# Edge-product tiles reordered by two engines in turn, and another pace for the edge scores in a four-layer graph network

## The chip, the cores and the metric

The kernel runs on one core of a Trainium2 chip. Its time is the device time in microseconds of one execution, here the median of three runs. The core has a matrix engine (TensorE, "PE" in the profile; its weight loads are "PEld"), a vector engine (VectorE, "DVE"), a scalar engine (ScalarE, "ACT"), a general engine (GpSimd, "POOL"), which here issues gathers and scatters as indirect DMAs, and SyncE ("SP"), which issues plain DMAs. Each engine works through its own queue in order. Tensors are laid over 128 partitions.

## The reference

Sixteen batches of 1024 nodes with 256 features pass through four layers over one adjacency matrix with few entries (about 17 a row). Everything is float32.

```python
# layer 0: a score for each edge, then sums over the edges
pre_u = einsum('bud,dk->buk', h, W1[:d]); pre_v = einsum('bvd,dk->bvk', h, W1[d:])
hidden = relu(pre_u[:, :, None, :] + pre_v[:, None, :, :] + b1)
S = sigmoid(einsum('buvk,ko->buvo', hidden, W2)[..., 0] + b2[0])
a = einsum('buv,bud->bvd', S * A, h)
m = einsum('uv,bud->bvd', A, h) * h
z = beta1*h + beta2*(a @ Wa + ba) + beta3*(m @ Wm + bm)
# layer 1
x = z + relu(einsum('ij,bjd->bid', A, z) @ W.T + b)
# layers 2 and 3 (attention, each with its own weights)
feats = x @ W1.T; f1 = feats @ W2 + b2
coefs = softmax(leaky_relu(f1[:, :, None] + f1[:, None, :]) + A, axis=-1)
x = coefs @ feats + bias2 + x
```

## The kernel before

The 16 batches are worked on in four groups of four (`GB = 4`). Node tiles have 128 rows (`NT = 8`).

**Edge scores.** Rather than score all 1024 × 1024 pairs, the kernel lists up to 32 neighbours of each node and scores those alone. `score_steps` (L717) is a generator with 608 steps after its first eight: a group has 8 node tiles × 16 slots and 6 extra tiles × 4 slots, so 152 steps. One step takes a tile of 128 × 1024 numbers (128 edges, four batches, 256 features each). GpSimd gathers it (L708, issued four steps ahead), VectorE adds the other side of the edge (L825) and applies relu and the weights (L827), and ScalarE sums each batch's 256 numbers (four operations, L831). After the last slot of a tile the sigmoid follows (L840 to L844), and its results wait in a list from which later steps scatter them, one or two a step (L713), into a dense array in DRAM, where the four batches of a pair of nodes lie side by side. L825 is `paced`: it waits until TensorE has done the product six before the place in the program where it stands.

**How the steps are dealt out.** `Side.along` (L888) runs a main generator, which yields nominal microseconds of TensorE work, and for each of them adds `PACE[stage]` to a debt. For each whole unit owed it issues one score step. The stages are `free` (work that needs no scores), `edges`, `one` (layer 1), `fronts` (projections of the attention layers) and `sums` (their weighted sums). Before a group's edge stage the program issues whatever steps are missing until that group is `finished`.

**The edge stage** (`with_edges`, L1120) multiplies the dense scores by each batch's transformed nodes (`hw`). It runs four column blocks `v` of 256 target nodes, and in each eight source tiles `ut`. For one tile SyncE loads `gd`, 128 × 256 nodes × 4 batches (512 KB, `load_gd`, four buffers), in which the batch is the innermost index. ScalarE copies it to `gc` with the batch outermost (L1129, two buffers, a read that hops four numbers each time), and TensorE runs eight products, which the profile shows as 16 matmul records. The eight sums of a block fill all eight PSUM banks. At the end of the block VectorE adds them to `z` (L1152, eight operations of 128 × 256), which frees the banks for the next block. A tile yields 3.4 nominal us (1 in the first block of group 0). In group 0 this stage also loads and exponentiates the adjacency (L1118). The first tiles of a group's edge stage are loaded ahead by `soon` (L1396) in the last sums of the group before.

**The layers of a group** (`group_layers`, L1355): layer 1 for two pairs of batches, then for each batch and attention layer a front (L1004, eight yields of 0.86) and two halves of sums (L1085, each eight yields of 1.7 and one of 1.2). A sums tile needs a VectorE operation `m` (L1099). The end of a sums half in the last layer reads four banks through L1325, L1326 and L1328, and only then are these banks free. Group 3's layers run with no score steps left; two of its four batches use lists for part of layer 1 (L1207, L1242, L1244).

The instructions of each engine are put in order when the program is built, by a scheduler that orders what is ready in its own estimate of the times; so the order on an engine isn't the order of the text. In group 2 at 2064.1 us, for example, L825 of a step runs ahead of a `gc` copy (2066.4 us), while that step's L831 follows it (2068.4 us).

Of the kernel before, what the change touches and what calls it, by code (L numbers as in the profile page):

```python
# [14 lines left out]
AF = mybir.ActivationFunctionType  # L15
# [5 lines left out]
BUFS = 2  # L21


PACE = dict(free=0.26, edges=0.225, one=0.288, fronts=0.255, sums=0.255)
SLOTS = 32
FIRST = 16
EXTRA = SLOTS - FIRST
# [16 lines left out]
def after(tc, ins, others, kind, why):  # L44
    dep = mybir.DependencyInfo(kind, mybir.DependencyReason.DATA)
    for o in others:
        tc.add_manual_dep(ins.ins, o.ins.name, dep, reason=why)
# [23 lines left out]
def gnn_stack_kernel(  # L71
# [27 lines left out]
    nc = tc.nc  # L99
# [13 lines left out]
    def bank():  # L113
        return psum[-1].tile([P, HN], F32, tag="bank", name="bank")
# [8 lines left out]
    def paced(ins, back=6):  # L123


        if recent:
            after(tc, ins, [recent[max(0, len(recent) - back)]], mybir.DependencyClass.Sync, "keeps pace")
        return ins

    def product(*args, **kw):  # L130
        recent.append(nc.tensor.matmul(*args, **kw))  # L131
        del recent[:-BACK]
        return recent[-1]
# [554 lines left out]
    with tc.If(listed > 0) as arm:  # L688
        with ExitStack() as stack:
# [192 lines left out]
            class Side:  # L882
# [4 lines left out]

                def along(self, main, pace=PACE):  # L888
                    for us in main:
                        self.owed += us * pace[doing[0]]  # L890
                        while self.owed >= 1:
                            self.owed -= 1
                            next(self.steps, None)
# [10 lines left out]
            def load_gd(g, v, ut, **pace):  # L904
                view = dense[g % BUFS][:DUMP].rearrange("(t p v) b -> t p v b", p=P, v=N)
                gd = gd_pool.tile([P, QN, GB], F32, tag="gd", name="gd")
                ins = nc.sync.dma_start(gd, view[ut][:, v * QN : (v + 1) * QN, :])
                put[g].before(paced(ins, **pace))
                return gd
# [207 lines left out]
            def exponential(jt):  # L1117
                paced(nc.scalar.activation(ea[:, jt, :], ea[:, jt, :], AF.Exp), 16)  # L1118

            def with_edges(g, hw, z):  # L1120

                doing[0] = "edges"
                for v in range(N // QN):
                    cols = slice(v * QN, (v + 1) * QN)
                    acc = [[bank() for _ in range(DH)] for _ in range(GB)]
                    for ut in range(NT):
                        gd = first_gd.pop(0) if first_gd else load_gd(g, v, ut, back=BACK)
                        gc = gc_pool.tile([P, GB, QN], F32, tag="gc", name="gc")
                        paced(nc.scalar.activation(gc, gd.rearrange("p n i -> p i n"), AF.Copy), 16)  # L1129
                        for i in range(GB):  # L1130
                            for eh in range(DH):
                                product(
                                    acc[i][eh][:, :QN], hw[i][:, ut, eh * P : (eh + 1) * P], gc[:, i, :],
                                    start=ut == 0, stop=ut == NT - 1,
                                )
                        if z_loads and ut % 2 == 0:
                            load, i = z_loads.pop(0)
                            paced(load(i), 12)
                        if (to_load or to_exp) and ut % 2 and v:
                            if v > 1 and to_exp:  # L1140
                                exponential(to_exp.pop(0))
                            if to_load:
                                jt = to_load.pop(0)
                                paced(nc.sync.dma_start(ea[:, jt, :], adjT_d[jt]), 16)
                                to_exp.append(jt)
                        yield 3.4 if g or v else 1
                    if v == N // QN - 1:
                        while to_exp:
                            exponential(to_exp.pop(0))
                    for i in range(GB):  # L1150
                        for eh in range(DH):
                            nc.vector.scalar_tensor_tensor(  # L1152
                                z[i][:, eh, cols], acc[i][eh][:, :QN], zbias[:, eh : eh + 1], z[i][:, eh, cols],
                                ALU.add, ALU.add,
                            )
# [245 lines left out]
            def far_ahead(z, main):  # L1401
# [6 lines left out]
                def slots():  # L1408
                    nonlocal gone
                    for us in itertools.chain(rest, main):  # L1410
                        gone += us
                        yield us * (0.68 if gone < 82 else 0.61)

                far.along(slots(), dict.fromkeys(PACE, 1))
                for _ in far.steps:
# [4 lines left out]
            for g in range(NGR):  # L1420
                hw, z = loaded.pop(0)
                while g not in finished:
                    next(side.steps)
                side.along(with_edges(g, hw, z))
                if g < NGR - 1:
                    side.along(group_layers(g, z))
                else:
                    for _ in far_ahead(z[2:], pair_layers(g * GB, z[:2], layer_one(z[:2]))):
                        pass
                    for _ in pair_layers(g * GB + 2, z[2:], from_lists(z[2:], msg)):  # L1430
                        pass
# [131 lines left out]
```

## Time and profile before

| | us |
|---|---|
| median of three runs (3133.77 to 3150.67) | 3143.56 |
| the profiled execution | 3123.2 |
| its span, first to last instruction | 3121.5 |
| TensorE matmuls busy | 3074.8 |
| VectorE busy | 2352.6 |
| ScalarE busy | 1945.1 |
| GpSimd busy | 1878.9 |

The mean granted TensorE clock was 0.998. The stages follow one another: work without scores up to about 942 us, then for each group its edge stage and its layers; group 0's edges begin at 942.1, group 1's at 1495.5, group 2's at 2045.3, group 3's at 2598.0 us. The 608 score steps run from 143.5 to 2547.8 us (first and last start of L825).

A row of the group view names line, engine, operation, what is written and read, shape and count; behind the bar stand busy time and mean ns of one, and then the engine's idle time ahead of these operations with what ended it. In the view of one tile's instructions a row gives duration as least/median/greatest in ns, and the first and last start. A row of the waits gives who waited for whom, total us, how often, and the longest. In the timeline a row is start, us, engine, line; like instructions close together are merged.

### The profile page before, as it was taken

To read this page: it belongs to the slowest core of one execution; us is meant where nothing else is said; L and a number is where in the kernel's file an instruction comes from. 1 tells how busy PE (TensorE), PEld (TensorE's weight loads), DVE (VectorE), ACT (ScalarE), POOL (GpSimd) and SP (SyncE) were. 2 spreads that over 40 slices of the span, in tenths; PEclk is the share of its full clock that TensorE was granted. 3 is DMA by queue.
4 is the path that set the end of the run, shared out by engine and by line. 5 is a ranking of instruction groups with operands and counts; after the bars stand their busy time and mean duration, and the time that the engine had idled before them with its cause. 6 is when DMAs were issued, how large, how long until landed. Compare 5 with 4: busy or idle time off the path is not lost. (4 is left out here: it accounts for less than half of the span.)

```text
span 3121.5 us, 39024 instructions
## 1 busy us (share of the span) xinstructions
PE 3074.8 (99%) x11954; PEld 2179.2 (70%) x11954; DVE 2352.6 (75%) x3183; ACT 1945.1 (62%) x6520; POOL 1878.9 (60%) x1483
## 2 busy tenths in 40 slices
PE   9999999999999999999999999999999999999999
PEld 5544555545547756888875688888568888858888
DVE  7887777768774678999667899966789982157844
ACT  3345565656667876787887677788667764414242
POOL 1156787777664577777666776766777770076600
PEclk9999999999999999999999999999999999999999
DMA  9998898888889776568877665887765565485500
GB/s 321 331 331 310 270 313 260 273 242 253 254 290 331 229 214 202 156 185 285 285 233 207 209 165 171 266 284 232 219 206 164 159 207 166 132 262 156 164 2 28
DMA packets 288420, 699.96 MB, mean 224 GB/s; under 512 B 46141, under 2 KB 141178, under 8 KB 281034
## 3 DMA queue, kind: packets, MB, share of 16 engines
q0 software_dynamic: 128224, 387.80, 42.5%
q1 hardware_dynamic: 132538, 258.46, 23.7%
q10 hardware_dynamic: 27440, 51.13, 4.3%
q8 instruction: 96, 1.57, 0.2%
q14 instruction: 122, 1.00, 0.1%
HBM read 565.83 MB, written 131.41 MB: 223 GB/s over the span
## 5 line engine op out<-in xcount | busy, mean ns | idle before, releaser
L831 ACT ACTIVATE z<-z 128x256 f32<-128x256 f32 x2432 | 979.0, 406 | 574.1 <-DVE z L827 549.0
L825 DVE TENSOR_TENSOR z<-z,u 128x1024 f32<-128x1024 f32 x608 | 738.9, 1220 | 374.8 <-PE bank L131 262.4
L131 PE MATMUL bank<-feats,m 128*128 128x257 f32 x4096 | 909.0, 380 | 0.7 <-ACT st L1325 0.5
L708 POOL DMA_INDIRECT z<-v_d,slot_v x512 | 662.2, 1293 | 376.0 <-ACT z L831 208.1
L131 PEld LDWEIGHTS bank<-feats,m 128*128 128x128 f32 x4096 | 769.4, 190 | 111.2 <-ACT st L1325 1.3
L713 POOL DMA_INDIRECT dense_d<-gt,slot_at x512 | 674.5, 1317 | 184.4 <-issue 130.3
L827 DVE SCALAR_TENSOR_TENSOR z<-z,w2r 128x1024 f32<-128x1024 f32 x608 | 737.3, 1219 | 9.0
L131 PE MATMUL bank<-gc,hw 128*128 128x256 f32 x2048 | 451.8, 382 | 15.6 <-ACT gc L1129 10.5
L831 ACT ACTIVATION_READ_ACCUMULATOR z<-z 128x1 f32 x2432 | 461.6, 190 | 0.0
L131 PE MATMUL bank<-adj_sb,h 128*128 128x512 f32 x1024 | 442.3, 592 | 3.3 <-ACT st L333 2.0
L131 PEld LDWEIGHTS bank<-gc,hw 128*128 128x128 f32 x2048 | 386.6, 190 | 80.2 <-ACT gc L1129 20.7
L1099 DVE SCALAR_TENSOR_TENSOR m<-rho,tau,adj_sb 128x512 f32<-128x512 f32 x512 | 375.8, 742 | 65.6 <-PE bank L131 62.7
L131 PE MATMUL bank<-adjT_in,y 128*128 128x512 f32 (+1 forms) x960 | 403.4, 581 | 6.0 <-DMA adjT_in<-adjT_d 5.9
L131 PEld LDWEIGHTS bank<-adj_sb,h 128*128 128x128 f32 x1024 | 194.3, 190 | 242.7 <-issue 237.5
L131 PEld LDWEIGHTS bank<-adjT_in,y 128*128 128x128 f32 x960 | 182.0, 191 | 221.0 <-issue 203.8
L131 PE MATMUL bank<-w,hT 128*128 128x512 f32 (+1 forms) x1024 | 334.9, 487 | 0.0
L1129 ACT ACTIVATE gc<-gd 128x1024 f32<-128x1024 f32 x128 | 264.7, 2069 | 88.4 <-PE bank L131 74.9
L131 PEld LDWEIGHTS bank<-w,hT 128*128 128x128 f32 x1024 | 194.8, 191 | 141.5 <-issue 118.4
L131 PE MATMUL bank<-g_wT,z 128*128 128x257 f32 x1024 | 231.4, 380 | 1.6 <-ACT st L1325 1.1
L131 PEld LDWEIGHTS bank<-g_wT,z 128*128 128x128 f32 x1024 | 191.8, 190 | 33.2 <-issue 3.1
L708 POOL DMA_INDIRECT z<-v_d,x_node x96 | 124.2, 1294 | 128.6 <-ACT z L831 96.6
L1152 DVE SCALAR_TENSOR_TENSOR z<-bank,zbias,z 128x256 f32<-128x256 f32 x128 | 54.6, 480 | 111.7 <-PE bank L131 111.4
(168 smaller groups left out, 2379.4 us busy)
## 6 DMA issues: line engine op xcount, KB each, us to landing
gd<-dense_d SPq DMA_DIRECT2D x128, 512.0 KB
dense_d<-zero ACTq DMA_DIRECT2D x64, 512.0 KB
adjT_in<-adjT_d SPq DMA_DIRECT2D x112, 256.0 KB
h<-in_x_dram SPq DMA_DIRECT2D x19, 1024.0 KB
u_d<-st SPq DMA_DIRECT2D x64, 256.0 KB
v_d<-st SPq DMA_DIRECT2D x64, 256.0 KB
hw_d<-st SPq DMA_DIRECT2D x64, 256.0 KB
u<-u_d POOLq DMA_DIRECT2D x32, 512.0 KB
```

The source lines that it names most:

```text
L131: recent.append(nc.tensor.matmul(*args, **kw))
L708: return nc.gpsimd.indirect_dma_start(out=dst, out_offset=None, in_=src[:], in_offset=bass.IndirectOffsetOnAxis(ap=at, axis=0), **how,)
L713: return nc.gpsimd.indirect_dma_start(out=dst[:], out_offset=bass.IndirectOffsetOnAxis(ap=at, axis=0), in_=src, in_offset=None,)
L825: paced(nc.vector.tensor_tensor(z, z, u, ALU.add))
L827: nc.vector.scalar_tensor_tensor(zk, zk, 0.0, w2r[:, None, :].to_broadcast([P, GB, D]), ALU.max, ALU.mult)
L831: nc.scalar.activation(zk[:, c, :], zk[:, c, :], AF.Copy, accum_out=s[:, k, c : c + 1])
L1099: nc.vector.scalar_tensor_tensor(m, r[:, cols], ta[:, kt : kt + 1], ea[:, kt, cols], ALU.max, ALU.mult)
L1129: paced(nc.scalar.activation(gc, gd.rearrange("p n i -> p i n"), AF.Copy), 16)
L1152: nc.vector.scalar_tensor_tensor(z[i][:, eh, cols], acc[i][eh][:, :QN], zbias[:, eh : eh + 1], z[i][:, eh, cols], ALU.add, ALU.add,)
```

## The change

Three of the five paces change, and the copy from `gd` to `gc` is made by VectorE for odd source tiles and by ScalarE for even ones. The wait that the copy carries (`paced(..., 16)`) stays the same.

```diff
-PACE = dict(free=0.26, edges=0.225, one=0.288, fronts=0.255, sums=0.255)
+PACE = dict(free=0.26, edges=0.255, one=0.288, fronts=0.265, sums=0.235)
...
                         gd = first_gd.pop(0) if first_gd else load_gd(g, v, ut, back=BACK)
                         gc = gc_pool.tile([P, GB, QN], F32, tag="gc", name="gc")
-                        paced(nc.scalar.activation(gc, gd.rearrange("p n i -> p i n"), AF.Copy), 16)
+                        by_batch = gd.rearrange("p n i -> p i n")
+                        if ut % 2:
+                            paced(nc.vector.tensor_copy(gc, by_batch), 16)
+                        else:
+                            paced(nc.scalar.activation(gc, by_batch, AF.Copy), 16)
```

## The prediction

> **What bounds the kernel now.** I read the page first, then the four runs of the edge product ("gc" matmuls) by their first and last start, then busy time by stage, then who waits for gc, and last VectorE's timeline at one turn of the column loop.
>
> ```profile
> PE 3074.8 (99%) x11954; PEld 2179.2 (70%) x11954; DVE 2352.6 (75%) x3183; ACT 1945.1 (62%) x6520; POOL 1878.9 (60%) x1483
> ```
>
> TensorE is the bound, but matmuls overlap in this count, so stalls hide in the 99%. The edge stages show them: each has the same 512 matmul records.
>
> ```profile
> L131 PE MATMUL bank<-gc,hw x512: 379/379/483, 942.1 to 1062.5; 128*128 128x256 f32 x171
> L131 PE MATMUL bank<-gc,hw x512: 379/379/483, 1495.5 to 1611.2; 128*128 128x256 f32 x171
> L131 PE MATMUL bank<-gc,hw x512: 379/379/634, 2045.3 to 2164.7; 128*128 128x256 f32 x171
> L131 PE MATMUL bank<-gc,hw x512: 379/379/382, 2598.0 to 2708.3; 128*128 128x256 f32 x171
> ```
>
> Lengths are 120.4, 115.7, 119.4 and 110.3 us. Group 3, with no score steps left, runs unhindered: 110.3/32 = 3.45 us for each node tile. The others lose 10.1 + 5.4 + 9.1 = 24.6 us. That is nearly all that this change can win.
>
> ```profile
> core 0: us, PE busy (x) PEld busy (x) DVE busy (x) ACT busy (x) POOL busy (x), PEclk, DMA share, GB/s
> 1063.00:1495.00 432.00, 431.04 (x1806) 328.73 (x1805) 396.26 (x541) 315.60 (x1190) 322.76 (x236) 1.00 0.69 209
> 1524.00:1611.00 87.00, 86.93 (x399) 74.83 (x399) 59.60 (x74) 82.11 (x187) 47.78 (x41) 1.00 0.81 260
> 2075.00:2165.00 90.00, 88.89 (x409) 76.74 (x408) 60.53 (x73) 83.22 (x189) 51.04 (x42) 1.00 0.82 263
> ```
>
> In the attention layers (first line) VectorE is 92% busy, yet TensorE idles 1 us: nothing is to be won there. In the edge stages ScalarE is the full engine (94%), VectorE has 32% free.
>
> ```profile
> L1129 ACT ACTIVATE gc<-gd 128x1024 f32<-128x1024 f32 x128 | 264.7, 2069 | 88.4 <-PE bank L131 74.9 <-DMA gd<-dense_d 12.8 <-ACT gc L1129 0.5
> L831 ACT ACTIVATE z<-z 128x256 f32<-128x256 f32 x2432 | 979.0, 406 | 574.1 <-DVE z L827 549.0 <-DVE share L1272 10.2 <-DVE mT L353 10.1
> L825 DVE TENSOR_TENSOR z<-z,u 128x1024 f32<-128x1024 f32 x608 | 738.9, 1220 | 374.8 <-PE bank L131 262.4 <-DMA z<-v_d,slot_v 62.7 <-ACT z L831 14.7
> L827 DVE SCALAR_TENSOR_TENSOR z<-z,w2r 128x1024 f32<-128x1024 f32 x608 | 737.3, 1219 | 9.0
> L1152 DVE SCALAR_TENSOR_TENSOR z<-bank,zbias,z 128x256 f32<-128x256 f32 x128 | 54.6, 480 | 111.7 <-PE bank L131 111.4
> L1078 ACT ACTIVATE rho<-rho 128x1024 f32<-128x1024 f32 x32 | 33.4, 1044 | 0.0
> L1242 DVE TENSOR_SCALAR msg<-z,slot_a 128x512 f32<-128x512 f32 x6 | 2.9, 486 | 0.4 <-PE bank L131 0.3
> ```
>
> The gathering read costs ScalarE 2069 ns against 1044 ns for a plain tile of that size. A score step is 1.22 + 1.22 = 2.44 us of VectorE and about 1.7 us of ScalarE (four times 0.41 us, the accumulator reads mostly beside). Who waits for gc:
>
> ```profile
> PE bank L131 <- ACT gc L1129: 10.5, 12, 2.2
> PEld bank L131 <- ACT gc L1129: 20.7, 31, 2.6
> PE bank L131 <- DVE st L1328: 4.3, 2, 2.8
> ```
>
> **Where the 24.6 us lie.** 4.3 us wait for L1328 and 0.7 for L1325, the end of the sums before, which frees banks; the granted clock was 0.94 over 30 us of group 2 (1.8 us). Three gaps of 2.18, 1.44 and 0.94 us (at 958, 963 and 1520 us) have ScalarE idle ahead of the copy: gd had not landed, so 4.6 us are the DMA's. This leaves 13 us that a busy ScalarE can answer for; I count 11.
>
> [...] L1242 needs 486 ns for 512 elements[...]. [...] Here every read of gc hops 16 bytes; no such large VectorE read is in this trace, ScalarE's doubling is the nearest. [...] The L1242 rows beside running gathers keep their 486 ns[...].
>
> **The change, part by part.**
>
> *Pace.* A step is issued for each 1/pace of a stage's nominal us. Edges: 4 × 8 × 3.4 = 108.8 nominal us, so 24.5 steps become 27.7 (+3.3). Sums: 16 × 14.8 = 236.8, times −0.020 = −4.7. Fronts: 64 × 0.86 = 55, times 0.01 = +0.6. A group ends some 1 step behind, group 0 (only 89.6 nominal us of edges) 1.5. All 608 steps still end within group 2, and each group's scores are complete well before its tiles load (group 2's last scatter goes 8 steps ahead, it was 10). So no forced run of steps appears. Relief in the sums is worth nothing, as TensorE doesn't stall there.
>
> *ScalarE in the edges.* A pair of tiles takes 6.91 us. Before: 2 × 2.07 + 1.53 × 1.7 = 6.7 us (97%; measured 94%). After: 2.07 + 1.73 × 1.7 = 5.0 us (73%). Its lateness goes: −11 us.
>
> *VectorE in the edges.* Before: 1.53 × 2.44 + 0.96 (L1152: eight of 0.48 in each eight tiles) = 4.7 us a pair (68%, as measured). After: 1.73 × 2.44 + 0.96 + c = 5.2 + c, with c the new copy. [...] it is 1.2 us as L827, plus ScalarE's extra of about 1.0 us: 2.2 us, the upper bound. [...] 1.25 us, which I take. A pair is then 6.4 of 6.91 us: it fits, hardly. Behind the copy queue only score steps, themselves held to TensorE's place; mid-block it starts about 0.5 us into the tile before its use and has 1.7 us to spare.
>
> *Where it doesn't fit.* The first copy of a column block after the prefetched one (tile 9, 17, 25: all odd, all VectorE's) meets the eight L1152 that free the banks:
>
> ```profile
> 1524.46 0.91 DVE L1152 SCALAR_TENSOR_TENSOR z<-bank,zbias,z 128x256 f32<-128x256 f32 x2 [4.85 <-PE bank L131]
> 1525.32 1.23 DVE L825 TENSOR_TENSOR z<-z,u 128x1024 f32<-128x1024 f32 x1
> 1526.46 0.48 DVE L1152 SCALAR_TENSOR_TENSOR z<-bank,zbias,z 128x256 f32<-128x256 f32 x1
> 1526.86 1.22 DVE L827 SCALAR_TENSOR_TENSOR z<-z,w2r 128x1024 f32<-128x1024 f32 x1
> 1527.99 2.04 DVE L1152 SCALAR_TENSOR_TENSOR z<-bank,zbias,z 128x256 f32<-128x256 f32 x5
> ```
>
> Tile 8 began at 1527.3 (two tiles after the gap at 1520); the last of these ends at 1530.03, 2.7 us in. A copy behind them ends at 2.7 + 1.25 = 3.95 us, 0.5 us late for 3.45; a copy ahead of them delays the last bank (due 3.0 us in) to 3.95, 0.9 us late. Nine such turns: 4.5 to 8.5 us, I take 6. It could be nothing if copy and steps change places.
>
> *DMA.* Three more steps in an edge stage add three gathers of 512 KB to a stage at a share of 0.81 to 0.88; the waits for gd may grow by 0 to 3 us: +1.
>
> Sum: −11 + 6 + 1 = −4 us on the profiled run's own 3123.2 us (span 3121.5, 1.7 around it): 3119. The runs' median is 20.4 us above that profile; moved alike, it comes to 3143.6 − 4 = 3139.
>
> **The rivals.**
>
> *A, faster.* Turns cost nothing, the stalls at the ends of sums go too since fewer steps crowd VectorE there (5 us), and the 20 us by which usual runs exceed the profile are partly the same lateness. For it: ScalarE at 94%, the only engine TensorE waits for here. Against: 6.4 us of DMA and clock stay. −11 − 5 − 5 = −21: 3122.
>
> *B, slower.* The strided copy on VectorE is slow. Above c = 6.91 − 5.2 = 1.7 us VectorE becomes the edges' bound. At 2.2 us a pair overruns by 0.5 us, 48 pairs in three groups: 24 us; turns add 2.7 + 2.2 − 3.45 = 1.45 × 9 = 13 us; less the 11 won: +26, 3169. For it: ScalarE's doubling[...]. Against: L1242's rate.
>
> *C, the new pace misplaces steps* against ends of sums, ±5 us by chance; it lies in the likeliest case's own range, 3129 to 3150.
>
> **How the numbers follow.** No change that can be told (a measurement of this kernel tells about 0.5%, 16 us): 0.42. A: 0.28. B: 0.30. The range 3118 to 3167 reaches nearly to A's and B's ends and leaves out about 2 in 10.
>
> **What would show it.** Right: VectorE's gc near 1.25 us, edge stages of about 114, 115 and 117 us, waits for ScalarE's gc near nothing, waits for L1152 or VectorE's gc at tiles 8, 9, 16, 17, 24, 25. Wrong: c above 1.7 us, VectorE near 100% in the edges, stages longer than before (B); or stages of 111 to 113 us (A); or new idle time of TensorE in sums or ahead of an edge stage.

## The result, and the profile after

The changed kernel takes 3129.74 us (median of 22 runs, 3120.36 to 3140.83); the kernel before, measured beside it, 3140.8 us (22 runs). The ratio is 0.9966, 95% interval [0.9954, 0.9977]. Repeated twice beside the experiments, the same kernel gave 0.9995 [0.9984, 1.0007] and 0.9997 [0.9988, 1.0005]. So the gain is 0.3% in one comparison and none that can be told in two: no change beyond 0.5%, as forecast. The kernel before itself had medians of 3140.8, 3129.1, 3126.0 and 3126.0 us in the four comparisons of this study, so kernels are compared below only by their ratio to the kernel before in the same comparison.

The busy times of the changed kernel, from the page:

```profile
PE 3071.5 (98%) x11954; PEld 2181.0 (70%) x11954; DVE 2422.3 (78%) x3247; ACT 1821.7 (58%) x6456; POOL 1894.7 (61%) x1483
```

ScalarE lost 123 us of work, VectorE gained 70. The span is 3122.0 us against 3121.5: in these two profiled executions nothing was won as a whole. Yet the stages moved. Edge product, changed kernel: the four stages one after the other, then the two kinds of copy (ns least/median/greatest, first and last start):

```profile
L131 PE MATMUL bank<-gc,hw x512: 379/379/797, 942.4 to 1063.2; 128*128 128x256 f32 x171
L131 PE MATMUL bank<-gc,hw x512: 379/379/483, 1496.6 to 1611.1; 128*128 128x256 f32 x171
L131 PE MATMUL bank<-gc,hw x512: 379/379/483, 2042.9 to 2157.1; 128*128 128x256 f32 x171
L131 PE MATMUL bank<-gc,hw x512: 379/379/792, 2594.6 to 2706.4; 128*128 128x256 f32 x171
...
L1133 ACT ACTIVATE gc<-gd x64: 2015/2084/2128, 934.6 to 2696.5; 128x1024 f32<-128x1024 f32 x64
L1131 DVE COPY gc<-gd x64: 1070/1116/1221, 945.0 to 2699.9; 128x1024 f32<-128x1024 f32 x64
```

Lengths are 120.8, 114.5, 114.2 and 111.8 us. Against the unhindered 110.3 the first three lose 18.6 us (24.6 before). Group 3, which lost nothing before, now loses 1.5. The copy costs VectorE 1.12 us.

Group 3's 1.5 us are the granted clock. It stood at 0.50 for 3.4 us just as the stage began, and its products started 0.43 us apart instead of 0.215 (the columns are explained at the next view; PEclk is the third number from the end):

```profile
2594.10:2597.50 3.40, 2.94 (x7) 2.41 (x8) 2.96 (x7) 1.49 (x5) 0.00 (x0) 0.50 1.01 367
```

The clock's record has other stretches at 0.50, of 3.4 or 6.8 us; in the edges of all profiles here each begins within 2 us of a wait of TensorE of 1 us or more. The changed kernel has one from 959.1 us (tile 4 of group 0, beside a wait of 2.9 us), the kernel before one from 2055.9 us (beside a wait of 2.8 us). One of 3.4 us costs 1.5 to 1.7 us, and the losses given below contain them.

Busy time by stage, changed kernel, edges of groups 1 and 2:

```profile
core 0: us, PE busy (x) PEld busy (x) DVE busy (x) ACT busy (x) POOL busy (x), PEclk, DMA share, GB/s
1497.00:1612.00 115.00, 112.52 (x515) 96.93 (x515) 97.13 (x113) 80.44 (x243) 85.73 (x64) 1.00 0.86 279
2043.00:2158.00 115.00, 112.88 (x517) 97.01 (x516) 98.56 (x115) 81.15 (x250) 86.95 (x66) 1.00 0.90 293
```

ScalarE is down from 94% to 70%, VectorE up from 68% to 85%; the DMA share of group 2 has risen to 0.90. Who makes TensorE wait in the edge product, over the whole changed kernel:

```profile
PEld bank L131 <- ACT gc L1133: 13.5, 9, 3.4
PE bank L131 <- ACT gc L1133: 10.2, 8, 3.2
PEld bank L131 <- DVE gc L1131: 6.1, 7, 1.7
PE bank L131 <- DVE gc L1131: 3.2, 4, 1.3
PEld bank L131 <- DVE z L1156: 1.2, 3, 0.7
```

The 10.2 us look like the 10.5 of before, but they are others. In the timelines I sorted the tiles by how late their first product starts (over 0.215 us after the product before it) and by what the copying engine did since `gc` became free. Where it sat idle until `gd` had landed I count 7.0 us (3.0 of them at tile 4 of group 0; 0.8 at tile 30 of group 1, where `gd` is only the likeliest reading); one wait of 1.2 us has ScalarE busy; 3.2 us stand ahead of group 3, which had no wait before. Counted in the same way the kernel before had 5.9 us for `gd` and 6.9 for a busy ScalarE (9.7 and, now, 1.3 for ScalarE with the small delays of a tile's other products).

Three further places changed. In group 2 the wait for the end of the sums (L1328, now L1332) is 0.2 us instead of 4.3. At the turns of the column loop VectorE's copy is late. And group 3 begins late. First a turn, on VectorE's timeline of the changed kernel, group 0, tile 17:

```profile
1000.74 0.92 DVE L1156 SCALAR_TENSOR_TENSOR z<-bank,zbias,z 128x256 f32<-128x256 f32 x2 [2.43 <-PE bank L131]
1001.65 1.23 DVE L825 TENSOR_TENSOR z<-z,u 128x1024 f32<-128x1024 f32 x1
1002.80 0.48 DVE L1156 SCALAR_TENSOR_TENSOR z<-bank,zbias,z 128x256 f32<-128x256 f32 x1
1003.19 1.22 DVE L827 SCALAR_TENSOR_TENSOR z<-z,w2r 128x1024 f32<-128x1024 f32 x1
1004.33 2.04 DVE L1156 SCALAR_TENSOR_TENSOR z<-bank,zbias,z 128x256 f32<-128x256 f32 x5
1006.29 1.21 DVE L825 TENSOR_TENSOR z<-z,u 128x1024 f32<-128x1024 f32 x1
1007.42 1.08 DVE L1131 COPY gc<-gd 128x1024 f32<-128x1024 f32 x1
```

It is the order the prediction drew, with one more L825 between the last bank and the copy. The copy ends at 1008.50, tile 17 starts at 1008.55, which is 1.43 us late. The bite differs from turn to turn: 1.43, 1.43, 0.64, 0.30 and 0.27 us here, with 0.96 us lost to banks at tiles 8 and 16 of group 2, 5.0 us in all.

Then the head of group 3. TensorE's waits in group 2's layers of the changed kernel:

```profile
PE bank L131 <- ACT gc L1133: 3.2, 1, 3.2
PE bank L131 <- DMA adjT_in<-adjT_d: 2.1, 2, 1.5
```

The last scores of group 3 (tile `gt`) in the changed kernel:

```profile
L713 POOL DMA_INDIRECT dense_d<-gt,slot_at x18: 965/1412/1497, 2531.7 to 2586.8; - x18
L844 DVE TENSOR_TENSOR gt<-s,slot_a x1: 219/219/219, 2562.6 to 2562.6; 128x64 f32<-128x64 f32 x1
```

The same of the kernel before:

```profile
L713 POOL DMA_INDIRECT dense_d<-gt,slot_at x20: 968/1357/2640, 2530.6 to 2577.6; - x20
L844 DVE TENSOR_TENSOR gt<-s,slot_a x1: 225/225/225, 2553.8 to 2553.8; 128x64 f32<-128x64 f32 x1
```

The last L844 is 8.8 us later although group 2's edges end 7.6 us earlier (2157.1 against 2164.7), and the last scatter is 9.2 us later. SyncE's loads of `gd` for group 3 wait for it, and start at 2589.0 instead of 2580.4. SyncE's waits for scatters around the head of group 3, changed kernel (8.0 us before):

```profile
SPq L907 <- DMA dense_d<-gt,slot_at: 23.5, 4, 15.9
```

The first product starts at 2594.6, 5.6 us after the first load is issued, and 3.2 us of that TensorE has waited for it. Before, 17.6 us lay between (2580.4 to 2598.0).

### The profile page after: what moved, and what is told of

Its sections match the earlier page's. It is cut to its first block, busy times and chain, and to the rows that moved or that the text cites. A ratio compares the mean times of both kernels' runs of the same rounds, so it can differ in the third digit from the quotient of the medians.

```text
span 3122.0 us, 39040 instructions
## 1 busy us (share of the span) xinstructions
PE 3071.5 (98%) x11954; PEld 2181.0 (70%) x11954; DVE 2422.3 (78%) x3247; ACT 1821.7 (58%) x6456; POOL 1894.7 (61%) x1483
## 5 line engine op out<-in xcount | busy, mean ns | idle before, releaser
L825 DVE TENSOR_TENSOR z<-z,u 128x1024 f32<-128x1024 f32 x608 | 738.3, 1219 | 299.1 <-PE bank L131 174.4
L713 POOL DMA_INDIRECT dense_d<-gt,slot_at x512 | 682.5, 1333 | 196.4 <-issue 139.3
L131 PE MATMUL bank<-gc,hw 128*128 128x256 f32 x2048 | 451.1, 382 | 14.9 <-ACT gc L1133 10.2
L1099 DVE SCALAR_TENSOR_TENSOR m<-rho,tau,adj_sb 128x512 f32<-128x512 f32 x512 | 375.7, 742 | 66.0 <-PE bank L131 61.7
L1133 ACT ACTIVATE gc<-gd 128x1024 f32<-128x1024 f32 x64 | 133.2, 2082 | 169.9 <-PE bank L131 104.2
L1131 DVE COPY gc<-gd 128x1024 f32<-128x1024 f32 x64 | 71.8, 1122 | 105.8 <-PE bank L131 79.3
```

What stands on the lines that cost most here:

```text
L713: return nc.gpsimd.indirect_dma_start(out=dst[:], out_offset=bass.IndirectOffsetOnAxis(ap=at, axis=0), in_=src, in_offset=None,)
L825: paced(nc.vector.tensor_tensor(z, z, u, ALU.add))
L1099: nc.vector.scalar_tensor_tensor(m, r[:, cols], ta[:, kt : kt + 1], ea[:, kt, cols], ALU.max, ALU.mult)
L1131: paced(nc.vector.tensor_copy(gc, by_batch), 16)
L1133: paced(nc.scalar.activation(gc, by_batch, AF.Copy), 16)
```

## The experiments

Theory 1: ScalarE's load in the edges is what costs TensorE time there; taking copies from it gains, the turns give part of it back, the pace is worth nothing. Theory 2: the gain is that of fewer steps in the sums. Theory 3: neither gains without the other. Ratios are to the kernel before in the same comparison, with the 95% interval. The diffs are against the changed kernel, unless the text says otherwise. "Loss" is the length of the first three edge stages, first to last start as above, less three times 110.3 us.

**The copy alone**, at the paces of before:

```diff
-PACE = dict(free=0.26, edges=0.255, one=0.288, fronts=0.265, sums=0.235)
+PACE = dict(free=0.26, edges=0.225, one=0.288, fronts=0.255, sums=0.255)
```

> The copies in turn, with the paces of before. Theory 1 (ScalarE's load in the edge stages is what is relieved; the pace is nearly nothing): all of the gain or more, ratio to before 0.995 to 0.998, edge stages of groups 0 to 2 shorter by 5 to 10 us in sum. Theory 2 (fewer steps in the sums is the gain): 0.999 to 1.001. Theory 3 (only both together gain, since the copy makes room that the pace fills): 0.998 to 1.000.

0.9994 [0.9983, 1.0005]; loss 24.0 us. Of ScalarE's own lateness little is left (about 2 us), but four turns cost 1.42 us each, the waits for `gd` and for the end of the sums (L1332 in group 2, 3.2 us) remain, and two stretches at clock 0.50 are in it (one before). The split by itself gains nothing that can be told, where Theory 1 had 0.2 to 0.5%.

**The paces alone**, with every copy on ScalarE:

```diff
-                        if ut % 2:
+                        if False:
```

> The new paces, all copies by ScalarE as before. Theory 1: ScalarE then needs 2 x 2.07 + 1.73 x 1.7 = 7.1 us for a pair of tiles of 6.91 us, so 48 pairs x 0.17 = 8 us slower, ratio 1.002 to 1.004, more waits of TensorE for ScalarE's gc. Theory 2: the gain without the copy, 0.996 to 0.998. Theory 3: 0.999 to 1.003.

1.003 [1.002, 1.004]; loss 29.9 us. The waits of TensorE over this kernel, then busy time in its edges of group 1 (columns as before: VectorE 82.18, ScalarE 108.81 of 115 us):

```profile
PEld bank L131 <- ACT gc L1133: 30.2, 44, 3.9
PE bank L131 <- ACT gc L1133: 16.2, 14, 3.5
```

```profile
1509.00:1624.00 115.00, 114.26 (x519) 96.36 (x518) 82.18 (x98) 108.81 (x262) 76.86 (x65) 1.00 0.87 284
```

ScalarE at 95% makes 16.2 us of waits where it made 10.5. Sorted as above, with all products of a tile, the delays behind a busy ScalarE grow from 9.7 to over 13 us, and three stretches at clock 0.50 cost 6.4 us instead of 1.6; the waits for the end of the sums shrink by about 5. So the new paces gain nothing without the split, as Theory 1 has it. This counts against Theory 2 but doesn't settle it, since the edges' pace rose too; the lower pace in the sums was not run alone.

**The even tiles by VectorE** instead of the odd ones, so that the copy at a turn stands at tiles 8, 16 and 24:

```diff
-                        if ut % 2:
+                        if ut % 2 == 0:
```

> As the changed kernel, but VectorE copies the even source tiles and ScalarE the odd ones, so that tiles 9, 17 and 25, the first ones after the banks are emptied, no longer stand behind VectorE's eight L1156. Theory 1 with its cost of these turns (6 us): ratio to before 0.994 to 0.996, no stall of TensorE at tiles 9, 17, 25. If the turns cost nothing: the changed kernel's 0.9966.

1.0024 [1.0012, 1.0036]; loss 27.9 us. As expected nothing stalls at the head of tiles 9, 17 and 25, but the ratio is worse than both expectations. TensorE now waits inside tiles 8, 16 and 24, for 1.2 to 3.0 us and once for 5.3 (1.7 of it at clock 0.50). VectorE's copy runs ahead of the eight L1156 there. Yet only 1.0 us of these waits ends with an L1156. The others end with ScalarE's copy of the next tile: the one in tile 24 of group 1 at 1594.34 us, 0.05 us after that copy and 1.0 us after the last L1156. So it isn't shown that the order at the turn makes them.

**A copy in memory order on ScalarE**, otherwise the kernel before (the order of the batches is left out):

```diff
-                        paced(nc.scalar.activation(gc, gd.rearrange("p n i -> p i n"), AF.Copy), 16)
+                        paced(nc.scalar.activation(
+                            gc.rearrange("p i n -> p (i n)"), gd.rearrange("p n i -> p (n i)"), AF.Copy
+                        ), 16)
```

> The kernel before, with the copy of gd to gc made by ScalarE in the order of memory: the change of order of the batches is left out, so layer 0's scored sums mix batches and the rest follows. It costs ScalarE about 1.05 us instead of 2.07 and VectorE nothing. Theory 1: ScalarE is relieved as much as by the change, with no turn cost: ratio 0.994 to 0.997, the waits of TensorE for gc down to those for the DMA. Theory 2: 1.000.

0.9954 [0.9939, 0.9968]; loss 10.1 us. The copies of this kernel:

```profile
L1129 ACT ACTIVATE gc<-gd x128: 1038/1057/1065, 932.2 to 2686.8; 128x1024 f32<-128x1024 f32 x128
```

Taking 1.01 us out of each ScalarE copy, with no work for VectorE, removes 14.5 of the 24.6 us. Not all of that was ScalarE's lateness. TensorE's waits of this kernel, where the one before has 10.5 and 4.3 us:

```profile
PE bank L131 <- ACT gc L1129: 3.9, 4, 1.5
PE bank L131 <- DVE st L1330: 1.9, 1, 1.9
```

Sorted as above, delays behind a busy ScalarE fall from 9.7 to 0.7 us, which is 9 of the 14.5. About 3 are the end of the sums, and 2 are waits for `gd`. So ScalarE's lateness is the largest part of the loss, less than the 11 to 13 that the prediction gave it, and what remains isn't its doing.

**The changed kernel again**, beside the next three:

> The changed kernel once more, beside the runs it is compared with. If its gain of 0.34% stands: ratio to before 0.995 to 0.998. If the first comparison was a lucky one: 0.998 to 1.000, like the copy alone (0.9994).

0.9995 [0.9984, 1.0007]; loss 18.2 us, and 3.7 us of waiting ahead of group 3. The trace repeats; the 0.3% do not.

**No VectorE copy at a turn**: tiles 3, 5 and 7 of each eight go to VectorE.

```diff
-                        if ut % 2:
+                        if ut in (3, 5, 7):
```

> As the changed kernel, but VectorE copies tiles 3, 5 and 7 of each block and ScalarE all others, tile 1 among them. In the trace of the copy alone the copy of tile 1 of a block stood behind eight L1156 and one L825 and came 1.4 us late, five times in three groups. Theory 1 (turn cost): those stalls go, ScalarE needs (5 x 2.07 + 8 x 0.87 x 1.7)/4 = 5.5 us of 6.91 a pair and isn't late: ratio 0.9935 to 0.996, edge stages of groups 0 to 2 lose at most 13 us in sum. Rival (the turn stalls are taken up by later slack, or ScalarE is late again): the changed kernel's ratio, or worse.

0.9999 [0.9989, 1.001]; loss 17.7 us. No copy at a turn waits behind L1156 any more, but the loss is that of the changed kernel: ScalarE has a tile more in each block and is late again at three tiles of group 0, 3.4 us in all, and once in group 2 (1.6 us), banks are late by 1.3 us, and `gd` is late by about 6 us (4 in the repeat beside it).

**The same with the paces of before** (this diff and the paces of the first experiment):

> The same with the paces of before. Theory 1: the turn was what ate the copy's gain, so 0.994 to 0.997 and close to the run with the new paces (within 0.2%). Theory 3 (the pace makes the gain, by making use of the room): about 0.999, and 0.3% over the run with the new paces.

0.999 [0.9979, 1.0]; loss 15.0 us, the least of all kernels that keep the order of the batches, and no wait ahead of group 3. The four stalls of 1.42 us at the turns are gone, 5.7 us, close to the 6 us that the prediction gave the turns. The rest of 24.0 - 15.0 = 9.0 us isn't theirs: the end of the sums takes 2.3 us less (L1332 0.9 instead of 3.2), and there is one stretch at clock 0.50 less (1.7 us). At the new paces the same removal brings only 0.5 us, and none if the clock is taken out (one such stretch in the repeat, none without turns). With the new paces the turns bite less (5.0 us in the changed kernel), and the higher pace in the edges costs elsewhere. Theory 1's ratio was missed here too; of Theory 3 the 0.999 came, but not the lead of the new paces, which are no faster.

**The new pace in the edges alone**, with the split:

```diff
-PACE = dict(free=0.26, edges=0.255, one=0.288, fronts=0.265, sums=0.235)
+PACE = dict(free=0.26, edges=0.255, one=0.288, fronts=0.255, sums=0.255)
```

> The changed kernel with only the edge pace raised (0.255), fronts and sums at 0.255 as before; groups then end some 3 steps further on. Theory 1: same as the changed kernel within 0.15%. Theory 2 (fewer steps in sums help at the ends of sums, where TensorE waits for banks): like the copy alone, 0.999 to 1.001, with more stall at the head of the edge stages of groups 1 and 2.

1.0038 [1.0024, 1.0051]; loss 24.2 us. Six turns bite in full here, 1.43 us each, and none of the waits ahead of group 3 appears. Both expectations are missed: the changed kernel beside it has 0.9995. With the split and the higher pace in the edges, the new paces of fronts and sums are worth 0.4%. The spans of the two profiles differ by 10.0 us: 6.0 more are lost in the edges, and the layers of groups 0 and 1 take 3.3 and 4.6 us longer, while group 2's layers and group 3's edges take 4.4 less. Group 1's layers, in this kernel and then in the repeat (columns as before):

```profile
1066.00:1495.00 429.00, 426.56 (x1782) 324.57 (x1781) 391.27 (x534) 311.30 (x1180) 321.37 (x232) 1.00 0.70 209
1066.00:1495.00 429.00, 429.00 (x1798) 328.23 (x1797) 388.06 (x533) 306.83 (x1159) 315.35 (x225) 1.00 0.69 206
```

So TensorE does idle in the layers here, 2.4 us in this stretch, and in the repeat it doesn't: 1.5 us are a wait for a load in layer 1, 1.0 are in the sums and at their ends. Over the whole kernel it waits 3.3 us for the `m` of a sums tile (L1099), 0.2 in the repeat. The profiled run, 3130.47 us, was the lowest of its five; what slowed the others further stays open.

**The changed kernel a third time**, beside the last three:

> The changed kernel once more, unaltered, on whatever chip the three beside it run on: the ratio to the kernel before was 0.9966 in the first comparison and 0.9995 in the second. If the gain is real and small (Theory 1: relief of ScalarE in the edges, partly given back at the turns and ahead of group 3), the ratio lies between 0.996 and 1.000 again; Theory 2 (the lower pace in sums is what gains) has no place for a gain any more. Edge stages of groups 0 to 2: a loss of 18 us together (18.4 and 18.0 in the two traces so far, 24.4 before). Ahead of group 3 again 3 to 4 us of waiting for the first copy. A ratio above 1.001 would mean that the first comparison was chance.

0.9997 [0.9988, 1.0005]; loss 17.6 us, and 3.4 us of waiting ahead of group 3. Of the expectation everything holds; the gain of the first comparison isn't confirmed. No stretch at clock 0.50 follows the wait ahead of group 3 here, and that group's edges take 110.4 us.

**All steps some four earlier**, to test the head of group 3:

```diff
-PACE = dict(free=0.26, edges=0.255, one=0.288, fronts=0.265, sums=0.235)
+PACE = dict(free=0.265, edges=0.255, one=0.288, fronts=0.265, sums=0.235)
```

> Pace of the stage without scores up from 0.26 to 0.265, so every later step stands some 4 steps earlier; all else as in the changed kernel. If TensorE's 3 to 4 us ahead of group 3 come from the last scores, which end some 5 us later since fewer steps go into the sums, then the last scatter is issued before about 2583 us (2586.8 in the changed kernel, 2577.6 before), no wait for the first copy of group 3 above 0.5 us is left, and the time is 3 to 4 us (0.1%) below the changed kernel's beside it. If that wait is due to something else (the copy's engine, the DMA's load there), it stays at 3 to 4 us. The edge losses of groups 0 to 2 stay near 18 us in either case.

1.005 [1.0032, 1.0067], slower, where 0.1% less than the changed kernel was expected; loss 21.0 us. In its group 2's layers TensorE waits only this:

```profile
PE bank L131 <- ACT st L1329: 0.5, 1, 0.5
```

The wait ahead of group 3 is gone, as it is in all kernels at the old paces, so it was the lateness of the last scores. (The last scatter was at 2590.9 us, which must be set against group 3's start at 2619.6: 28.7 us ahead instead of 7.8. As a date, "before 2583", the expectation was wrong, since everything before it had become later.) But the first stage, which I had taken to have room, grew: the edges begin at 967.7 us, 14.0 later than in the repeat beside it. Waits of this kernel before 965 us:

```profile
ACT st L333 <- DMA hw_d<-st: 57.3, 15, 10.8
...
PE bank L131 <- DVE mT L353: 15.0, 6, 5.0
...
PE bank L131 <- ACT st L333: 8.9, 5, 3.3
```

The same in the repeat beside it:

```profile
ACT st L333 <- DMA hw_d<-st: 41.5, 19, 9.7
...
PE bank L131 <- DVE mT L353: 11.0, 4, 2.9
...
PE bank L131 <- ACT st L333: 2.1, 1, 2.1
```

The longest of them, on VectorE's timeline of the slower kernel, and TensorE's product that waited:

```profile
496.14 1.22 DVE L825 TENSOR_TENSOR z<-z,u 128x1024 f32<-128x1024 f32 x1 [3.52 <-DMA z<-v_d,slot_v]
497.28 2.35 DVE L827 SCALAR_TENSOR_TENSOR z<-z,w2r 128x1024 f32<-128x1024 f32 x2
499.55 0.68 DVE L353 TENSOR_TENSOR mT<-bank,hT 128x512 f32<-128x512 f32 x1
...
500.29 2.07 PE L131 MATMUL bank<-mT,wm 128*128 128x512 f32 x2 [5.04 <-DVE mT L353]
```

VectorE stood 3.5 us before the L825 of a step whose gather wasn't there, and L353, which TensorE's product needs, came behind that step. At all five waits for L333 ScalarE in turn had stood 2.3 to 10.8 us before it, since its buffer wasn't stored yet. The longer waits on L353 and L333 amount to 11 us, most of the 14. Why more of them fall together at this pace wasn't tried.

**A copy in memory order on VectorE**, otherwise the changed kernel:

```diff
-                            paced(nc.vector.tensor_copy(gc, by_batch), 16)
+                            paced(nc.vector.tensor_copy(
+                                gc.rearrange("p i n -> p (i n)"), gd.rearrange("p n i -> p (n i)")
+                            ), 16)
```

> The changed kernel with VectorE's copies in memory order, for odd tiles; the order of the batches is left out there, so those tiles are multiplied with the wrong batches. It measures what the hop of 16 bytes costs VectorE: 1.12 us with it; I expect 0.70 to 0.75 us without it[...]. If the turns' stalls are due to the eight L1156 and the L825 ahead of the copy, and not to the copy's own length, each of them shrinks by some 0.4 us, from 1.42 to about 1.0, and the edge loss of groups 0 to 2 falls by 2 to 3 us, to about 15.5; the ratio to the changed kernel beside it is 0.999 to 1.000. If VectorE's whole load in the edges is the trouble, the loss falls by more, to 12 or below.

0.9983 [0.9972, 0.9994]; loss 18.8 us. The copies of this kernel:

```profile
L1131 DVE COPY gc<-gd x64: 681/693/929, 953.6 to 2708.2; 128x1024 f32<-128x1024 f32 x64
```

So the hop costs VectorE 0.4 us a copy (1.12 us with it, 0.69 without; the 0.70 to 0.75 expected was an estimate of mine whose basis no trace had shown). Where a turn bit 1.43 us it now bites 1.04 and 0.94, which is the shorter copy and no more: the eight L1156 and the L825 ahead are the rest. The loss as a whole didn't fall to the 15.5 expected; 4.4 us of late `gd` at tiles 4 and 12 of group 0, and one wait of 2.2 us at tile 5 of group 2, stood against it, and a second stretch at clock 0.50 in the edges (1.7 us). It didn't fall to 12 or below either, which speaks against VectorE's whole load as the trouble.

**Every copy on VectorE**, at the paces of before:

```diff
-PACE = dict(free=0.26, edges=0.255, one=0.288, fronts=0.265, sums=0.235)
+PACE = dict(free=0.26, edges=0.225, one=0.288, fronts=0.255, sums=0.255)
...
-                        if ut % 2:
+                        if True:
```

> The paces of before, and VectorE makes every copy, ScalarE none. VectorE then has, for a pair of tiles, 1.53 x 2.44 + 0.96 + 2 x 1.12 = 6.9 of 6.91 us: rival B of the prediction made true by number instead of by slowness. If VectorE's capacity decides, TensorE waits for VectorE's copies in all tiles, not at the turns alone, the edge loss of groups 0 to 2 goes above that of before (24.4 us), to 30 to 45 us, and the ratio is 1.003 to 1.007. If only the turns matter, the loss is 2 x the 1.42 us x 9 or so, hence at most 25 us, and the ratio is within 0.001 of 1.

1.0004 [0.9992, 1.0016]; loss 18.0 us. Busy time in its edges of groups 1 and 2:

```profile
1497.00:1617.00 120.00, 114.21 (x514) 97.44 (x514) 106.03 (x127) 47.90 (x215) 90.53 (x58) 0.99 0.81 261
2053.00:2166.00 113.00, 111.10 (x511) 96.51 (x512) 103.93 (x118) 44.60 (x203) 83.51 (x60) 1.00 0.86 279
```

VectorE at 88 and 92% makes no general wait: the stalls stand at turns (four of 1.42 us, with 0.55 us for banks before each), where `gd` is late (3.2 us in group 0), and at tile 2 of groups 1 and 2 (2.4 and 0.5 us). 25 steps ran in each of the two stages, as at the old pace they should, so nothing was put off. The sum of 6.9 us for a pair was too high: 25 × 2.44 + 32 × 1.12 + 32 × 0.48 = 112 us, but VectorE is busy only 104 to 106 us in the stages. The timeline shows why. Neighbours in its queue overlap: a copy of 1.13 us starts at 1546.00 and the L825 behind it at 1547.05.

Of the three theories none holds whole. ScalarE's load does cost TensorE time in the edges (Theory 1), but handing half of its copies to VectorE brings nothing that can be told in the total; and the lower pace in the sums has worth only beside the other two changes (0.4%, one comparison).

No version that computes the same beats both kernels by more than the interval. The best, three VectorE copies a block at the old paces, has 0.999 [0.9979, 1.0], beside which the changed kernel had 0.9995. The experiments divide the time by stages like this ("layers" is from the last edge product of a group to the first of the next):

| | loss, edges 0 to 2 | layers of group 1 | layers of group 2 | edges of group 3 |
|---|---|---|---|---|
| before | 24.6 | 434.1 | 433.3 | 110.3 |
| copy alone | 24.0 | 435.1 | 433.5 | 110.3 |
| edges' pace, split | 24.2 | 436.3 | 432.8 | 110.3 |
| no turn, old paces | 15.0 | 435.8 | 434.4 | 110.2 |
| all on VectorE, old paces | 18.0 | 436.2 | 434.5 | 110.2 |
| changed | 18.6 | 431.8 | 437.5 | 111.8 |
| changed, second | 18.2 | 431.7 | 435.4 | 112.1 |
| changed, third | 17.6 | 431.8 | 437.0 | 110.4 |
| paces alone | 29.9 | 432.0 | 436.4 | 113.8 |
| no turn, new paces | 17.7 | 431.8 | 436.0 | 113.7 |
| even tiles on VectorE, new paces | 27.9 | 431.7 | 434.2 | 114.5 |
| memory order on ScalarE, old paces | 10.1 | 432.6 | 433.3 | 110.3 |
| memory order on VectorE, new paces | 18.8 | 431.8 | 435.8 | 112.1 |
| all steps earlier | 21.0 | 433.7 | 431.8 | 110.3 |

The lower pace in the sums can be read in the two middle columns. With 0.235 group 1's layers take 432.0 us or less in all kernels but the last, with 0.255 they take 432.6 to 436.3. Group 2's layers look longer with 0.235, but most of that is the wait ahead of group 3: in the last row, without it, they take 431.8. In the last column every value above 111 us has a stretch at clock 0.50 in it, of 3.4 or 6.8 us.

## Why the prediction was right, point by point

No change that can be told was forecast, and none came. The forecast of 3139 us lay 9 us above the first median and 13 to 16 above the repeats, whose kernel before was itself 17.6 us below the three runs that the forecast was anchored to; as a ratio, 0.9987 (-4 of 3143.6 us), it lies between the first comparison and the repeats. The mechanism was right in the edges, with one size too large, and incomplete outside them. That the total came so near is partly luck: of the parts that the prediction had put at nothing, some turned out to save 6.8 us and some to cost 5.7.

- *ScalarE's lateness, -11 us.* Right in kind, too large. Delays behind a busy ScalarE, with all products of a tile, were 9.7 us and are 1.3: -8.4. The 11 to 13 were a remainder, and one term before it was too small: at tile 13 of group 0 (992.3 us) TensorE idled another 0.7 us after ScalarE had stood 2.4 us until `gd` landed, which the 4.6 us for the DMA leave out.
- *VectorE's copy, 1.25 us taken.* The 1.25 was my estimate; no trace of the kernel before shows a VectorE copy with such a read. It measures 1.12, well below the break-even of 1.7 on which rival B rested. The price of B was not met, and with every copy on VectorE, the sum that B took for the limit (6.91 us a pair), there is still no general wait: sums of durations overstate VectorE's load by 6 to 8%. With GpSimd busy three quarters of the edges, the 64 copies took 1.07 to 1.22 us.
- *Turns, +6 us.* 5.0 us measured. The place and the queue were right; the size of one was not. A full bite is 1.43 us and not 0.5 to 0.9, as an L825 often stands between the last L1156 and the copy; fewer than nine turns bite.
- *DMA, +1.* Counted in one way, from 5.9 to 7.0 us: +1.1.
- *Edge stages of 114, 115 and 117 us.* 120.8, 114.5 and 114.2: the sum 349.5 for 346. The excess is group 0, where tile 4 alone lost 4.5 us (3.0 for a late `gd`, 1.5 at clock 0.50). The prediction's own three lengths don't fit its sum: they are 9.5 us below the 355.5 of before, where it forecasts -4. The stages give -6.0.
- *"Relief in the sums is worth nothing, as TensorE doesn't stall there".* This step failed. With the edges' pace raised and the sums' left, TensorE waits 3.3 us for tiles of the sums (L1099); with both changed it waits 0.2 us. The stalls at the ends of sums eased as well: L1328's 4.3 us in group 2 fell to 0.2, the 5 us of rival A. That the pace did this isn't shown: L1328 (L1330, L1332) is below 1 us in all kernels at 0.235, but at 0.255 it ranges from nothing to 4.3.
- *"Each group's scores are complete well before its tiles load".* Wrong for group 3, and the error of the working is plain: I worked out the margin of group 2, in steps, and took it for every group. Behind group 3's last step there are no more steps, and its last tile still sends 16 scatters (L713), which end 24 us after its L844 (2562.6 to 2586.8). From the last scatter to group 3's first product 20.4 us were left before (2577.6 to 2598.0) and 7.8 are now, and TensorE waits 3.2 to 3.7 us in each of the three profiles of the changed kernel. The kernel with all steps earlier shows that this is the cause. The prediction had named such idle time ahead of an edge stage as a sign that it was wrong; it came beside the signs that it was right.

So the sum for the edges reads, in place of -11 + 6 + 1 = -4: ScalarE -8.4, turns +5.0, DMA +1.1, the ends of the sums (L1328 and L1325) -4.5, together -6.8, where the stages show -6.0; the 0.8 us between are mostly delays of 0.1 us and less, behind VectorE's late copies. Beside it, not foreseen, group 1's layers -2.3, group 2's layers with the head of group 3 +4.2, and group 3's edges +1.5 (all from the table). That is -2.6 us in the profiled pair; its spans differ by +0.5, and the rest is in stages that the change doesn't touch, most of it (2.4 us) in the last layers. These vary by more than that between kernels with the same paces, so I draw nothing from it.

Rival C was the nearest to what the pace does. At the new paces the loss is 5 to 6 us lower with the odd tiles on VectorE (24.0 to between 17.6 and 18.6), 2.7 us higher without copies at the turns (15.0 to 17.7), and 5 higher with all copies on ScalarE (24.6 to 29.9); the clock's stretches are 2 us of the first and most of the last. Which steps stand at which turn, and why fewer bite, wasn't tried. Whether the first comparison's 0.3% is more than chance stays open as well: the edges' gain repeats in all three traces, the total does not, and the first stage alone, whose pace isn't changed, gave 942.4, 944.3 and 953.7 us until the first edge product in three profiles of the changed kernel.

## What to carry to other kernels

Before moving an operation to an engine with room, look at what stands in that engine's queue at the moment the operation is due, not at its mean share: VectorE at 92% made TensorE wait at much the same few places as at 85%, mostly the turns, behind eight bank reads. A paced background task has a deadline at its end; follow it to its last transfer, here 16 scatters after the last step, before slowing it. Count a loss in the same way before and after, and look at the granted clock behind each long wait. And compare the changed kernel more than once: a gain of 0.3% with a tight interval was not there on two other occasions.

## What the runs showed of the hardware

With a read that hops 16 bytes between numbers, a ScalarE copy of 128 x 1024 numbers took 2.07 us (the kernel before), in memory order 1.06. A VectorE copy took 1.12 us with the hop (the changed kernel) and 0.69 in memory order. VectorE was thus 1.8 times as fast as ScalarE with the hop and 1.5 times without it. How VectorE reads such an operand, and so where its 0.4 us come from, was not shown.

The granted TensorE clock fell to 0.50 for 3.4 or 6.8 us beside some waits of TensorE: in the changed kernel beside those of 2.9 and 3.2 us, at 959.1 and 2594.1 us. It didn't beside every one: in the third profile of the same kernel it stayed at 1.00 after a wait of 3.4 us ahead of group 3. With the 3.2 us at 2594.1 came 1.5 us more in this way, about half as much again.
